# Batch 0's gate and up products as seven block products, with the weight sums made as the second slot opens

## The chip, the cores and the metric

The kernel runs on one core of a Trainium2 chip. The metric is the device time of one execution in microseconds (us), the median over several executions; smaller is better. PE is the matrix engine, PEld its weight loads, DVE the vector engine, ACT the scalar engine, POOL GpSimd, and SP the engine that issues most of the DMA transfers.

## The reference

A pre-norm block on four batches of 512 tokens, all in 32-bit floats: `x` is 4 x 512 x 512, 32 query heads and 8 key/value heads of 16, and a gated layer with 1376 hidden columns.

```python
x = x + attn(layernorm(x), Wq, Wk, Wv, Wo)    # rotary embedding, causal softmax, 4 query heads for a key head
x = x + ffn(layernorm(x), W_gate, W_up, W_down)

def ffn(x, W_gate, W_up, W_down):
    up = x @ W_up.T
    gate = silu(x @ W_gate.T)
    return gate * up @ W_down.T
```

## The kernel before

**Slots.** Attention is done in 32 groups (batch, one of four sets of heads, one of two halves), eight groups to a batch. `slot(b, steps)` runs the eight groups of batch `b`, and puts other work of PE, as steps with an estimated cost each, into gaps between the parts of a group: after each of four visits, and (from slot 1 on) after the group's `averages`. `fill` takes steps from the list until the slot's share is used up; a step of cost zero (`after`) rides along, so its place in the list is its place in every engine's queue. All engines run their instructions in the order of the program, SP too: a transfer that must wait holds up every transfer behind it.

**What stands in the gaps.** In slot 0: projections of the batches 1 to 3. In slot 1: the output projection and second layernorm of batch 0 (`attended(0)`), the last of the query projections of batch 3, then batch 0's gated layer and half of its down products. In slot 2: the rest of batch 0's down products, batch 1's output projection, batch 1's gated layer and half of its down products; in slot 3 the same for batch 2. What is left (batch 3) runs behind the last slot with nothing beside it: the tail.

**The gated layer, two ways.** The 1376 hidden columns are ten blocks of 128 (`whole = 10`) and an edge of 96. Batch 0 goes through `hidden`: for each block and each of gate and up, four products over the 512 inputs, 512 tokens wide; its weights come from `load_f`, two blocks ahead. The batches 1 to 3 go through `seven`: ten units, `u` even for gate and odd for up, each of 256 hidden columns x 512 inputs x 512 tokens, done with Strassen's scheme in Winograd's form, seven block products in place of eight. A unit has seven steps (`a1, y1, y2, v1, v2, w1, w2`), each with two products 256 tokens wide. It needs four sums of the activations (`sums_of`, DVE, into `sums`, which lies in `xnTs[1]`) and the weights in seven blocks (`packed[u]` in DRAM: three blocks copied as they are, four sums made from them). It adds its results together on DVE (L687, L696, L697, L705), and silu is a tanh on ACT (L666), a DVE step (L667) that `owed` puts into the next unit, and a product with up (L670; on POOL inside the slots, on DVE in the tail). `hidden` has instead a tanh and two DVE steps for each block (L561, L562, L564).

**The weight blocks.** `packs(u)` makes `packed[u]` in slot 1, beside batch 0's layer: `load` brings 512 KB to `spare` (in `xnTs[1]`) and copies the 384 KB of unchanged blocks from DRAM to DRAM (L587, L588); `combine` is four additions on POOL (L592 to L595); `store` writes 512 KB (L598). In slots 2 and 3 and in the tail a unit's blocks come by four loads (L621, 896 KB a unit), issued during the unit before.

**The edge and its moves.** The 96 last columns are done by `hidden` in all batches, for the batches 1 to 3 ahead of the units. Its last step moves three corners of 32 x 128 by SP (L566, `home<-home`), which wait for DVE's L564. `seven` puts all four sums between the edge's two halves.

**Inside the slots** `narrow` is set, and each product is cut into four strips of 32 output columns that run side by side on PE. The profile has two records for each of these matmuls: a 512-wide product is 8 records, a 256-wide one 8.

**Causal masking** of the exponentials is done by POOL (`causal`, L861) ahead of `averages` (L883) on PE; `greatest` (L801) on DVE has to read a score bank before PE writes it again (L755, L768).

Of the kernel before, what the change touches and what calls it, by code (L numbers as in the profile page):

```python
# [74 lines left out]
def preln_block_kernel(  # L75
# [52 lines left out]
    shared = flat[:, : 24 * P].rearrange("p (a b k m) -> p a b k m", a=3, b=2, k=NK)  # L128
    wq_sb = flat[:, : NK * D].rearrange("p (k m) -> p k m", k=NK)
    wk_sb, wv_sb = shared[:, 2, 0, :, :], shared[:, 2, 1, :, :]  # L130
# [36 lines left out]
    spare = turn.rearrange("p (u f m) -> p u f m", u=2, f=4)  # L167
    rest_w = rope_sb[:, : 2 * NK * 96].rearrange("p (a k m) -> p a k m", a=2, k=NK)
    once = rope_sb[:, 2 * NK * 96 : 2 * T]
# [330 lines left out]
    wgu = {}  # L500

    def load_f(c):

        if c >= NF or c in wgu:
            return
        f = c % NF
        n = min(P, FF - f * P)
        t = shared[:, (c + 2) % 3, :, :, :]
        for a, w in enumerate((wg, wu)):
            load_w(t[:, a, :, :n], w[:, f * P : f * P + n])  # L510
        wgu[c] = t

    def hidden(b, n, owed=None):

        gs = {}

        def half(f, a):
            def weights(a):
                return rest_w[:, a] if owed else wgu[f][:, a]

            m = min(P, FF - f * P)
            most = T - P
            cols = slice(0, T if m == P else most)

            def product(ps, k):
                if a == 0 and k == 0 and not owed:
                    load_f(f + 2)
                if m == P:
                    product_of(ps, weights(a)[:, k, :], xnTs[0][:, k, :], k == 0, k == NK - 1)
                    return  # L530


                for q in range(3):
                    at = slice(32 * q, 32 * q + 32)
                    nc.tensor.matmul(  # L535
                        ps[at, :most],
                        lhsT=weights(a)[:, k, at],
                        rhs=xnTs[0][:, k, :most],
                        start=k == 0,
                        stop=k == NK - 1,  # L540
                    )
                for q, kq in (divmod(n, NK) for n in range(3 * k, 3 * k + 3)):
                    nc.tensor.matmul(  # L543
                        ps[96:P, ts(q, P)],
                        lhsT=weights(a)[:, kq, 32 * q : 32 * q + 32],
                        rhs=xnTs[0][:, kq, most:],
                        start=kq == 0,
                        stop=kq == NK - 1,
                    )

            def finish(ps):
                return [(0.69, lambda: gated(ps))]

            def gated(ps):
                if owed:
                    owed()
                if a == 0:
                    gs[f] = scratch()

                    g = gs[f][:, cols]  # L560
                    nc.scalar.activation(g, ps[:, cols], AF.Tanh, scale=0.5)  # L561
                    nc.vector.scalar_tensor_tensor(g, g, 1.0, ps[:, cols], ALU.add, ALU.mult)  # L562
                else:
                    nc.vector.tensor_tensor(homes[n][:, f, cols], ps[:, cols], gs[f][:, cols], ALU.mult)  # L564
                    for q in range(3) if m < P else ():
                        nc.sync.dma_start(  # L566
                            out=homes[n][32 * q : 32 * q + 32, f, most:], in_=homes[n][96:P, f, ts(q, P)]
                        )

            return [(1.72 if m == P else 1.29, step) for step in portions([lambda ps, k=k: product(ps, k) for k in range(NK)], finish)]  # L570

        return [step for f in range(NF - 1 if owed else 0, NF) for a in range(2) for step in half(f, a)]
# [4 lines left out]
    def packs(u):  # L577
# [3 lines left out]
        t, columns = spare[:, u % 2], w.rearrange("(k p) m -> p k m", p=P)  # L581

        def load():
            for i in range(2):
                load_w(t[:, 2 * i : 2 * i + 2, :].rearrange("p f (k m) -> p (f k) m", k=2), w[:, at + P - P * i :][:, :P])
            raw = packed[u].rearrange("p f (k m) -> p (f k) m", k=2)
            nc.sync.dma_start(out=raw[:, :4, :], in_=columns[:, :, at + P : at + 2 * P])  # L587
            nc.sync.dma_start(out=raw[:, 4:6, :], in_=columns[:, 2:, at : at + P])  # L588
# [12 lines left out]

    def load_rest():
        for a, w in enumerate((wg, wu)):
            load_w(rest_w[:, a, :, :], w[:, whole * P :])


    places = {"a": (0, (0,)), "y": (256, (1, 3)), "v": (1280, (5, 6)), "w": (2304, (2, 4))}
# [8 lines left out]
    def load_blocks(kind, v):  # L616
        if v >= (B - 1) * whole:
            return
# [4 lines left out]
    def first_blocks():  # L623
        for kind in "ayvw":
            load_blocks(kind, 0)

    def sums_of():
# [3 lines left out]
        for out_, one, other in ((t3, b22, b12), (t1, b12, b11), (t2, b22, t1), (t4, b21, t2)):  # L631
            nc.vector.tensor_tensor(out_, one, other, ALU.subtract)  # L632

    def seven(b, n):
# [6 lines left out]
        def owed():  # L641
            while carried:
                carried.popleft()()
# [505 lines left out]
```

## Time and profile before

| what | us |
|---|---|
| three runs: median, lowest to highest | 865.3, 864.68 to 866.2 |
| the profiled execution: its time | 863.93 |
| its span, first to last instruction | 862.2 |
| DVE, ACT, POOL busy over the span | 535.9, 217.2, 292.5 |

The granted clock of PE was 0.999 of full speed over the span. The slots can be told in the trace by the groups of `averages` (L883): slot 0 ends at about 174 us, slot 1 at 357, slot 2 at 538, slot 3 at 710; then the tail runs to 862. "Busy" is the time in which an engine had at least one instruction running, and a wait is put down to what was released last.

```profile
L562 DVE SCALAR_TENSOR_TENSOR u<-u,mm 128x512 f32<-128x512 f32 x10 | 6.9, 688 | 14.9 <-ACT u L561 14.9
L705 DVE TENSOR_TENSOR u<-mm,u 128x512 f32<-128x512 f32 x15 | 10.3, 684 | 4.0 <-PE mm L269 2.9 <-PE mm L272 1.2
L697 DVE TENSOR_TENSOR u<-mm,u 128x256 f32<-128x256 f32 x15 | 6.4, 424 | 0.5
L670 POOL TENSOR_TENSOR home<-home,u 128x512 f32<-128x512 f32 x20 | 25.2, 1281 | 25.5 <-DVE u L705 25.3
L592 POOL TENSOR_TENSOR xnT<-xnT 128x256 f32<-128x256 f32 x10 | 7.3, 728 | 0.2
```

These are groups of instructions by line and shape: line, engine, operation, tiles (out<-in), shapes, count, then busy time, mean nanoseconds of one, and the idle time of the engine just before them with what ended it.

### The profile page before, as it was taken

What the parts mean: (1) busy time and instruction counts of PE and PEld (TensorE: products, weight loads), DVE (VectorE), ACT (ScalarE), POOL (GpSimd) and SP (SyncE); (2) the same over time, 40 slices, a digit from 0 to 9 for tenths busy, and PEclk for the clock granted to TensorE, in tenths of its full rate; (3) what the DMA queues carried; (4) which work ended last, traced back from release to release, by engine and by line L of the source; (5) the groups of instructions that cost most, each with busy time, mean ns of one, the idle gap of its engine ahead of it and who ended that gap; (6) DMA issues with size and microseconds to landing.
All of it is one profiled execution on the core that took longest, in us unless ns stands there. A gap on an engine that the chain in (4) does not pass through costs nothing.

```text
span 862.2 us, 26973 instructions
## 1 busy us (share of the span) xinstructions
PE 836.6 (97%) x11446; PEld 419.9 (49%) x11446; DVE 535.9 (62%) x1593; ACT 217.2 (25%) x296; POOL 292.5 (34%) x418
## 2 busy tenths in 40 slices
PE   6999999999999999999999999999999999999998
PEld 5654444544333335333655543334555544478843
DVE  7887788778555554467777774586777433256620
ACT  1034434422222222222332332222333420011100
POOL 4565565664343444222233341231233331000000
PEclk9999999999999999999999999999999999999999
DMA  8500114004866753534233320132432402445300
GB/s 255 135 6 4 53 17 88 5 4 106 285 185 194 201 174 107 182 114 107 62 116 103 91 87 14 64 52 76 121 102 89 131 15 73 104 138 152 105 12 36
DMA packets 134519, 85.50 MB, mean 99 GB/s; under 512 B 60320, under 2 KB 121376, under 8 KB 134144
## 3 DMA queue, kind: packets, MB, share of 16 engines
q1 hardware_dynamic: 134112, 78.02, 32.4%
q10 hardware_dynamic: 288, 5.77, 1.7%
q8 instruction: 90, 1.47, 0.7%
q14 instruction: 29, 0.24, 0.1%
HBM read 64.95 MB, written 22.54 MB: 101 GB/s over the span
## 4 chain that ended last, share of the span: by engine, by line
PE 76%; DVE 12%; POOL 3%; DMA 3%; issue 2%; ACT 2%; SPq 1%; POOLq 0%; DVEq 0%; ACTq 0%
PE mm L272 37%; PE mm L269 15%; PE sc L755 12%; DVE junk L801 7%; PE av L883 6%; PE sc L768 4%; POOL e L861 2%; PE mm L543 1%; ACT e L856 1%; DMA shared<-packed 1%; DVE rot L331 1%; DVE st L219 1%; PE mm L535 1%; DVE xnT L632 1%; DMA lowest<-turned 1%
## 5 line engine op out<-in xcount | busy, mean ns | idle before, releaser
L801 DVE CUSTOM_DVE_ANT_0 junk<-sc,mask 128x128 f32<-128x128 f32 (+3 forms) x512 | 251.1, 490 | 142.8 <-PE sc L768 83.8
L856 ACT ACTIVATE e<-sc 128x1024 f32<-128x1024 f32 (+1 forms) x192 | 165.4, 881 | 378.6 <-PE sc L768 308.4
L272 PE MATMUL mm<-xnT,shared 128*32 128x256 f32 (+1 forms) x3520 | 244.7, 420 | 1.4 <-DVE xnT L280 1.0
L861 POOL TENSOR_SCALAR_AFFINE_SELECT e<-e 128x512 f32<-128x512 f32 (+2 forms) x192 | 106.8, 566 | 269.5 <-ACT e L856 266.4
L272 PEld LDWEIGHTS mm<-xnT,shared 128*32 128x32 f32 x3520 | 117.0, 110 | 112.5 <-issue 61.8
L755 PE MATMUL sc<-home,qa 32*64 32x512 f32 (+6 forms) x2048 | 158.1, 421 | 6.1 <-DVE low L801 3.5
L768 PE MATMUL sc<-qa,home 32*64 32x512 f32 (+6 forms) x2048 | 152.3, 427 | 3.9 <-DVE low L801 3.3
L755 PEld LDWEIGHTS sc<-home,qa 32*64 32x64 f32 x2048 | 67.3, 131 | 94.9 <-issue 32.7
L272 PE MATMUL mm<-wd_sb,home 128*32 128x512 f32 (+1 forms) x808 | 93.7, 595 | 0.0
L883 PE MATMUL av<-e,home 128*32 128x512 f32 (+3 forms) x1024 | 82.3, 438 | 1.7 <-POOL e L861 1.6
L269 PE MATMUL mm<-xnT,shared 128*128 128x256 f32 x360 | 79.9, 382 | 1.9 <-DMA shared<-packed 1.9
L269 PEld LDWEIGHTS mm<-xnT,shared 128*128 128x128 f32 x360 | 68.0, 191 | 13.7 <-issue 4.5
L768 PEld LDWEIGHTS sc<-qa,home 32*64 32x64 f32 x2048 | 58.8, 130 | 28.5 <-DVE low L801 10.5
L269 PE MATMUL mm<-wd_sb,home 128*128 128x512 f32 (+1 forms) x150 | 65.0, 593 | 0.0
L724 DVE SCALAR_TENSOR_TENSOR xr<-mm,xr 128x512 f32<-128x512 f32 x16 | 11.0, 687 | 71.5 <-PE mm L269 54.9
L883 PEld LDWEIGHTS av<-e,home 128*32 128x32 f32 x1024 | 30.9, 109 | 47.0 <-issue 35.7
L272 PEld LDWEIGHTS mm<-wd_sb,home 128*32 128x32 f32 (+1 forms) x808 | 27.0, 110 | 50.6 <-issue 48.8
L269 PEld LDWEIGHTS mm<-wd_sb,home 128*128 128x128 f32 (+1 forms) x150 | 28.4, 190 | 35.8 <-issue 35.8
L272 PE MATMUL mm<-wo_sb,cx 128*32 128x512 f32 x384 | 44.9, 595 | 0.0
L801 DVE DVE_READ_ACCUMULATOR2_ANT low<- 128x1 f32 x512 | 42.3, 83 | 0.0
L222 POOL TENSOR_TENSOR rstd<-rstd,neghalf 128x1 f32<-128x1 f32 x32 | 20.4, 639 | 60.3 <-DVE rstd L221 59.8
L907 POOL TENSOR_TENSOR inv<-us,inverse 128x256 f32<-128x256 f32 x32 | 20.6, 645 | 49.6 <-DVE inverse L900 48.4
(112 smaller groups left out, 670.3 us busy)
## 6 DMA issues: line engine op xcount, KB each, us to landing
shared<-packed SPq DMA_DIRECT2D x90, 256.0 KB
flip<-u SPq DMA_DIRECT2D x88, 64.0 KB
packed<-xnT SPq DMA_DIRECT2D x10, 512.0 KB
xnT<-flip SPq DMA_DIRECT2D x18, 256.0 KB
xr<-in_x SPq DMA_DIRECT2D x16, 256.0 KB
out<-xr SPq DMA_DIRECT2D x16, 256.0 KB
shared<-packed SPq DMA_DIRECT2D x30, 128.0 KB
xa<-in_x SPq DMA_DIRECT2D x12, 256.0 KB
```

The costliest lines, as they stand in the source:

```text
L219: nc.vector.bn_stats(st, src)
L222: nc.gpsimd.tensor_tensor(rstd, rstd, neghalf, ALU.pow)
L269: nc.tensor.matmul(out, lhsT=lhsT, rhs=rhs, start=start, stop=stop)
L272: nc.tensor.matmul(out[c : c + 32], lhsT=lhsT[:, c : c + 32], rhs=rhs, start=start, stop=stop)
L724: nc.vector.scalar_tensor_tensor(xr[b, i], py[i], 0.5, xr[b, i], ALU.mult, ALU.add)
L755: nc.tensor.matmul(dst[at : at + 64, :n], lhsT=qa[g][rows_of(r), q : q + 64], rhs=keys_of(g)[rows_of(r), :n], start=True, stop=True,)
L768: nc.tensor.matmul(dst[at : at + 64, first_q:], lhsT=keys_of(g)[rows_of(r), k : k + 64], rhs=qa[g][rows_of(r), P * j + first_q :], start=True,
L801: nc.vector.tensor_tensor_reduce(out=junk[:, :n], in0=src, in1=mask[:, T - n : T] if i else mask[:, T:], scale=-1.0, scalar=BIG, op0=ALU.a ...
L856: nc.scalar.activation(dst, src, AF.Exp, scale=1.0 / math.sqrt(DH))
L861: nc.gpsimd.affine_select(out=e[rows, heads, c : c + P], in_=e[rows, heads, c : c + P], compare_op=ALU.is_ge, fill=0.0, base=base, pattern ...
L883: nc.tensor.matmul(av[32 * r : 32 * r + 32, P * j :], lhsT=v[:, j, 4 * (m // 2) + r, DH * (1 - hf) : DH * (3 - hf)], rhs=e[:, r, c : c + n ...
L907: nc.gpsimd.tensor_tensor(us[m][:, :, hf, :], turned[0][:, :, hf, :], by, ALU.mult)
```

## The change

1. Batch 0 goes through `seven` too. `hidden` and `load_f` are gone; the edge has a function of its own (`edge`), which comes behind the units for batch 0 and ahead of them for the others. Batch 0 keeps `once` in the unused last part of its home tile, since the other place still holds rotary tables.
2. The sums of weights have to be there earlier. The unchanged blocks are copied in slot 0 (`copies`, 20 transfers). `load`, `combine` and `store` start when slot 1 opens and follow a timetable (`timed`) of one pack in 4.5 units of estimated cost. They use `homes[0][:, 4:10]`, free after slot 0, three packs in turn, in place of `xnTs[1]`.
3. The four sums of activations are four steps, each between other steps; `owed` gives out one silu step at a time (in `y1` and in `v1`) in place of two in `y2`.
4. The edge's moves wait in a queue (`moves`) and are issued later: in step 12 of the units for the batches 1 to 3, in the down products for batch 0.
5. Places in the flat weight buffer are arranged anew, so that unit 0's `a` and `y` blocks can be loaded early in slot 1 and `v` and `w` behind the last query projection.

```diff
-    wk_sb, wv_sb = shared[:, 2, 0, :, :], shared[:, 2, 1, :, :]
+    wk_sb, wv_sb = (flat[:, n * NK * P : (n + 1) * NK * P].rearrange("p (k m) -> p k m", k=NK) for n in (4, 5))
...
-    spare = turn.rearrange("p (u f m) -> p u f m", u=2, f=4)
...
-    def load_f(c):
...
-    def hidden(b, n, owed=None):
...
+    moves = deque()
+
+    def moved():
+        while moves:
+            moves.popleft()()
+
+    def edge(n):
+        home, f, most, gs = homes[n], whole, T - P, []
+
+        def product(ps, a, k):
...
+        def gated(ps, a):
+            if a == 0:
+                gs.append(scratch()[:, :most])
+                g = gs[0]
+                nc.scalar.activation(g, ps[:, :most], AF.Tanh, scale=0.5)
+                nc.vector.scalar_tensor_tensor(g, g, 1.0, ps[:, :most], ALU.add, ALU.mult)
+                return
+            nc.vector.tensor_tensor(home[:, f, :most], ps[:, :most], gs[0], ALU.mult)
+            for q in range(3):
+                moves.append(
+                    lambda q=q: nc.sync.dma_start(
+                        out=home[32 * q : 32 * q + 32, f, most:], in_=home[96:P, f, ts(q, P)]
+                    )
+                )
...
     def packs(u):
-        t, columns = spare[:, u % 2], w.rearrange("(k p) m -> p k m", p=P)
+        t = homes[0][:, 4 + 2 * (u % 3) : 6 + 2 * (u % 3), :].rearrange("p a (f m) -> p (a f) m", m=2 * P)
         def load():
...
-            raw = packed[u].rearrange("p f (k m) -> p (f k) m", k=2)
-            nc.sync.dma_start(out=raw[:, :4, :], in_=columns[:, :, at + P : at + 2 * P])
-            nc.sync.dma_start(out=raw[:, 4:6, :], in_=columns[:, 2:, at : at + P])
...
+    def copies(u):
+        at = 2 * P * (u // 2)
+        columns = (wg, wu)[u % 2].rearrange("(k p) m -> p k m", p=P)
+        raw = packed[u].rearrange("p f (k m) -> p (f k) m", k=2)
+        nc.sync.dma_start(out=raw[:, :4, :], in_=columns[:, :, at + P : at + 2 * P])
+        nc.sync.dma_start(out=raw[:, 4:6, :], in_=columns[:, 2:, at : at + P])
...
-    places = {"a": (0, (0,)), "y": (256, (1, 3)), "v": (1280, (5, 6)), "w": (2304, (2, 4))}
+    places = {"v": (0, (5, 6)), "w": (1024, (2, 4)), "y": (2048, (1, 3)), "a": (3072, (0,))}
...
-    def sums_of():
+    def sums_of(which):
         t1, t2, t3, t4 = (sums[:, n] for n in range(4))
-        for out_, one, other in ((t3, b22, b12), (t1, b12, b11), (t2, b22, t1), (t4, b21, t2)):
-            nc.vector.tensor_tensor(out_, one, other, ALU.subtract)
+        one, two, by = ((t1, b12, b11), (t2, b22, t1), (t3, b22, b12), (t4, b21, t2))[which]
+        nc.vector.tensor_tensor(one, two, by, ALU.subtract)
...
     def seven(b, n):
+        once = rope_sb[:, 2 * NK * 96 : 2 * T] if b else home[:, whole, : 2 * P]
         def owed():
-            while carried:
+            if carried:
                 carried.popleft()()
...
-        edge = hidden(b, n, owed)
-        return [*edge[:2], after(sums_of), *edge[2:], *steps]
+        t = [after(lambda s=s: sums_of(s)) for s in range(4)]
+        if b == 0:
+            return [t[0], t[1], steps[0], t[2], steps[1], t[3], *steps[2:], *edge(n)]
+        ends = edge(n)
+        return [ends[0], t[0], ends[1], t[1], ends[2], t[2], ends[3], t[3], *steps[:12], after(moved), *steps[12:]]
...
+    early = [*rest1[16:-8], *turns, begin3, *rest2, *turned3, *rest3[:-24]]
+    for u in range(whole):
+        early.insert(4 * u + 4, after(lambda u=u: copies(u)))
+    slot(0, early)
...
+    tiles[3:3] = [after(moved)]
+    cut += 1
...
+    asides = []
+    for u in range(whole):
+        load, combine, store = packs(u)
+        asides += [(max(4.5 * u - 2.5, 0.2 * u), load), (4.5 * u + 5, combine), (4.5 * u + 8, store)]
+    start1 = [before[0], *rest3[-24:-12], *before[1:], *rest3[-12:-1], *behind, rest3[-1]]
+    layer = seven(0, 0)
+    blocks = [after(lambda kind=kind: load_blocks(kind, 0)) for kind in "vw"]
+    asides += [(13.0, lambda: load_blocks("a", 0)), (13.0, lambda: load_blocks("y", 0))]
+    layer = [*layer[:8], after(spilled), *layer[8:36], after(load_rest), after(load_down), *layer[36:]]
+    slot(1, timed([*start1, *blocks, *layer, *tiles[:cut]], asides))
```

`timed(steps, asides)` puts each aside ahead of the first step at which the summed cost has reached its time. The units of the batches 1 to 3, their loads and the slots 2 and 3 are otherwise as they were.

## The prediction, made before the changed kernel ran

> **What bounds the kernel now.** I read the busy times of the whole page first, then the same by slot, then what PE waited for, then the blocks in which the changed products run.
>
> ```profile
> PE 836.6 (97%) x11446; PEld 419.9 (49%) x11446; DVE 535.9 (62%) x1593; ACT 217.2 (25%) x296; POOL 292.5 (34%) x418
> ```
> ```profile
> core 0: us, PE busy (x) PEld busy (x) DVE busy (x) ACT busy (x) POOL busy (x), PEclk, DMA share, GB/s
> 174.30:357.20 182.90, 180.45 (x2502) 69.59 (x2504) 105.76 (x345) 48.44 (x60) 81.95 (x121) 1.00 0.53 159
> 357.20:538.20 181.00, 180.70 (x2980) 85.54 (x2976) 122.32 (x369) 50.55 (x69) 52.23 (x78) 1.00 0.32 94
> 538.20:710.20 172.00, 168.99 (x2788) 82.44 (x2784) 108.49 (x305) 50.00 (x69) 51.31 (x75) 1.00 0.29 81
> 710.20:862.20 152.00, 146.31 (x576) 93.11 (x566) 59.44 (x100) 9.51 (x21) 3.51 (x5) 1.00 0.31 88
> ```
>
> These rows are slot 1, slot 2, slot 3 and the tail. PE is the bound in all: slot 1, which the change rebuilds, has it busy for 180.45 of 182.90 us. Slot 2 already runs a layer by `seven` inside the gaps and loses only 0.3 us. So PE time taken from slot 1 shortens the run, unless a wait comes in its place. What PE waits for, in slot 1 (first fence) and from 538 us on (second):
>
> ```profile
> PE av L883 <- POOL e L861: 1.2, 3, 0.5
> PE mm L272 <- DVE xnT L280: 1.0, 1, 1.0
> ```
> ```profile
> PE mm L269 <- DMA shared<-packed: 1.9, 1, 1.9
> PE sc L768 <- DVE low L801: 1.7, 1, 1.7
> PE sc L755 <- DVE low L801: 0.8, 2, 0.4
> ```
>
> Each line: total us, times, longest. All of them lie at places that the change touches.
>
> **Step 1, the products: -8.2 us.** Four blocks of the timeline, two of each kind (start, us, form, records):
>
> ```profile
> 223.90 1.93 PE L272 MATMUL mm<-xnT,shared 128*32 128x512 f32 x16
> 226.80 3.64 PE L272 MATMUL mm<-xnT,shared 128*32 128x512 f32 x32
> 428.23 2.80 PE L272 MATMUL mm<-xnT,shared 128*32 128x256 f32 x48
> 435.67 3.66 PE L272 MATMUL mm<-xnT,shared 128*32 128x256 f32 x64
> ```
>
> Sixteen more records of 512 columns (two products) cost 3.64 - 1.93 = 1.71 us; sixteen of 256 (one step of a unit) 3.66 - 2.80 = 0.86. What a block has beyond that (0.22) is paid once for each gap, and the number of gaps stays. `hidden` has 10 blocks x 2 x 4 products x 8 records = 640 records: 40 x 1.71 = 68.4 us. `seven` has 10 x 7 steps of 16: 70 x 0.86 = 60.2. The edge and the down products are the same. The shorter products load as many weights for half the columns; slot 2 does just that at the pace above, PEld at 85.54 of 181 us, so I add nothing.
>
> **Step 2, DVE and ACT in slot 1: no cost beside PE, but for the opening.** Taken out: ten L562 and ten L564 of 0.688 us, 13.8. Put in, by the rows of slots 2 and 3: ten each of L687, L696, L705 (0.687, 0.688, 0.684) and L697 (0.424), 24.8; ten L667 (0.768), 7.7; four sums (0.68 to 0.80), 3.0. DVE goes from 105.8 to about 127.5 us in a slot of some 178: 72%, beside 68% in slot 2. ACT gets ten tanh (0.622) in place of ten (0.597), and ten copies to `once` (0.364): +3.9 on 48. The cover is PE's own time; without it all of DVE's 21.7 would count.
> At the opening of the layer the cover is thin. After `averages` DVE has L897 and L900 (0.68 + 0.25), then two sums (1.4) that `y2` needs, 2.3 us, while PE has two steps (1.8): 0.5 of wait. `v1` stands behind a third step and a score block (2.8 + 1.04 = 3.8 us), and its weights are issued only when the last query projection has read the buffer and `lowest` has gone, some 1.5 us in: with a landing like the tail's (3.29, below) 4.8, with the 4.55 of 656.3 us in the chain of waits 6.1. I take 1.2 for both together; bounds 0 (SP early) and 2.3. In turn, L280's 1.0 goes: the transposed tiles are now needed one gap later, behind `averages`.
>
> **Step 3, POOL: +3.6 us.** The packs' four additions are as many as before, but come closer together, and ten products L670 (1.28 us each, 12.8) join them in slot 1: about 95 of 178 us. The total is harmless; the place is not. One group of slot 1 before, on POOL, and PE behind it:
>
> ```profile
> 282.06 1.91 POOL L861 TENSOR_SCALAR_AFFINE_SELECT e<-e 128x512 f32<-128x512 f32 x3 [8.41 <-ACT e L856]
> 284.06 0.73 POOL L592 TENSOR_TENSOR xnT<-xnT 128x256 f32<-128x256 f32 x1
> 286.48 0.73 POOL L595 TENSOR_TENSOR xnT<-xnT 128x256 f32<-128x256 f32 x1
> 287.16 0.76 POOL L861 TENSOR_SCALAR_AFFINE_SELECT e<-e 128x256 f32<-128x256 f32 x2
> ```
> ```profile
> 287.62 0.77 PE L883 MATMUL av<-e,home 128*32 128x256 f32 x6 [0.50 <-POOL e L861]
> ```
>
> Mask, a combination (284.06 to 287.21), the last mask, and PE waits 0.50. In the changed program's order three groups have a combination at this place: pack 4 as here (0.5); pack 1 in the group with two rstd steps (the mask at 194.17 comes about 1.0 later, on top of 0.21: 1.2); and pack 7 with both products of unit 1 ahead of it, 2 x 1.28 = 2.56 more: 3.1. Sum 4.8, less the 1.2 of now: +3.6. Bounds: -1.2 (no mask late) and three times 3.1 less 1.2 = +8.1. Behind the late mask stands only `qa` for the group after next.
> [...]
>
> **Step 4, SP and the transfers.** Slot 0 gets 20 DRAM copies of 0.62 us issue each, in its first three groups. SP idles there (54.8 to 66.3 us and 70.5 to 82.4, between `qa` and `lowest`), eight copies (5 us) fit in each; the last four delay the `xa` loads at 86.84 by 2.5 us: landed at 92.0 (2.68 as at the start), first read at 93.46. Nothing; without that cover some 1 us on DVE. In slot 1 SP has by its order: store of pack u, loads of a later pack, and a unit's blocks between them. A unit takes 7 steps, 10 us with the attention between, and its blocks are asked for a unit ahead. Landing takes 3.3 to 4.6, a store waits for POOL up to 3.2. That fits. The load in the stretch of packs, units and the spill together will be about that of 215 to 235 us now (DMA share 0.81 to 0.90), where PE lost nothing. I take 0; bounds 0 and the second rival.
> [...]
>
> **Step 5, moves and sums in the later layers: -2.9 us.** In the tail SP stood at the moves until DVE's L564 was done, and only then asked for unit 1's blocks (SP's timeline, then the chain of waits):
>
> ```profile
> 759.53 1.84 SPq L566 DMA_DIRECT2D home<-home  x3
> ```
> ```profile
> 762.62 3.29 DMA shared<-packed
> ```
>
> PE stood until 766.04, the 1.9 above. With the moves 12 steps later SP is free from 753.6 (after `out`), `a` waits only for `a1` at about 758.3 and lands before 764.1: -1.9 (bounds -1.9 and 0). The 1.7 in slot 3 (600.3 us) follows four sums in one run (596.8 to 600.2) ahead of `greatest`. Now a PE step lies between any two, but two or three still fall in one gap: -1.0, bounds 0 and -2.5 (all waits for L801 there). `owed` one by one makes the same work smoother, 0.
>
> **Sum.** -8.2 - 1.0 + 1.2 + 3.6 - 1.0 - 1.9 = -7.3. Against the profiled execution: 863.9 - 7.3 = 856.6. Its time is 1.4 below the median of the runs; with that, 858.0.
>
> **Rivals.**
> *All cover holds* (for it: slot 2 loses 0.3 us with the same units): no new waits, 865.3 - 8.2 - 1.0 - 1.2 - 2.5 - 1.9 = 850.5. Against it: slot 2 has no packs on POOL.
> *SP becomes the bound in slot 1: slower.* Packs 4 to 9 are still under way while units run. A block load stands behind a store that waits for POOL (3.2 here) and a pack load that waits for an older store to land; the longest wait of SP for a stored pack is now 7.7 us. 3.2 + 7.7 + a landing of 3.3 is 14.2 against 10 us of lead: 4 us for a unit. With four units late, 16 on -7.3: 874. It decides against the kernel once the lead is missed by more than 1.8 us in each of four units. Against it: 7.7 was seen once, beside the 2.5 MB of down weights, which now come after the packs.
> *DVE becomes the bound:* each of the four groups with units pays a wait like slot 3's 1.7: +6.8, 864.8, no change. For it: 77% busy (16.87 of 22 us) from 446 to 468 us. Against it: PE lost 0.27 there.
> *Strassen is not in effect for batch 0, or costs 8 products:* then only steps 3 to 5 remain, about 866. The program's order shows the 70 steps, so it gets next to nothing.
>
> **How the numbers follow.** Forecast 0.72, all cover 0.10, SP 0.11, DVE 0.07, the last under 0.01. Faster by over 0.2% (1.7 us, about what a measurement of this kernel can tell from no change) are the first two: 0.82; slower is the SP case, 0.11; same is DVE's, 0.07. The likeliest case's own range is 854 to 862. To leave out no more than 2 in 10 I reach to 853 (into the case of full cover) and 863.5 (POOL near its upper bound, or half of DVE's case).
>
> **What would show it.** Right: no records of 512 columns for mm<-xnT,shared in narrow strips, 70 steps at 0.86; slot 1 at about 178.5 us (182.9 - 8.2 - 1.0 + 1.2 + 3.6); PE's wait for L861 in slot 1 at 3 to 5 us, the largest in the group where L670 and a combination meet; no wait of L269 for `packed` in the tail. Wrong: PE waiting for `packed` in slot 1 over 2 us, waits for L801 in slot 1 over 3 us, a slot 0 longer than 174.3, or slots 2 and 3 changed by more than 3.

## The result, and the profile after

The changed kernel takes 872.8 us (median; 872.54 to 875.07) against 865.5 us of the kernel before on the same chip: a ratio of 1.009, with a 95% interval of 1.0071 to 1.0109. The forecast was 858.0 us with a range from 853 to 863.5, so the sign was wrong. The profiled executions are 8.8 us apart (872.76 and 863.93, spans 871.05 and 862.22).

First the same view by slot as before: slot 1, slot 2, slot 3 and the tail, cut at the end of each slot's last `averages`.

```profile
core 0: us, PE busy (x) PEld busy (x) DVE busy (x) ACT busy (x) POOL busy (x), PEclk, DMA share, GB/s
176.14:370.94 194.80, 177.39 (x2981) 88.60 (x2984) 128.29 (x379) 51.06 (x70) 97.04 (x130) 0.97 0.48 147
370.94:551.88 180.94, 180.64 (x2980) 85.51 (x2976) 121.93 (x369) 50.55 (x69) 52.67 (x78) 1.00 0.32 94
551.88:721.14 169.26, 168.74 (x2789) 82.27 (x2784) 106.91 (x305) 50.02 (x69) 50.53 (x75) 1.00 0.30 83
721.14:871.05 149.91, 146.05 (x574) 93.14 (x566) 59.48 (x100) 9.39 (x21) 3.51 (x5) 1.00 0.31 89
```

Cut at the same places, the kernel before has 182.65, 180.95, 172.10 and 152.00 us. So slot 0 is 1.6 us longer, slot 1 12.2 longer, slot 2 the same, slot 3 2.8 shorter and the tail 2.1 shorter: together 8.8. The whole loss is in slot 1, and its row has a column to look at that the prediction never used: PEclk is 0.97 there and 1.00 everywhere else.

What PE waited for in slot 1 (waits: total us, times, longest):

```profile
PE mm L269 <- DMA shared<-packed: 11.7, 5, 5.1
PE av L864 <- POOL e L842: 4.6, 3, 2.8
PE mm L269 <- DVE xnT L608: 1.0, 1, 1.0
```

In the same stretch the kernel before waited 1.2 us for the mask and 1.0 for L280. From 551 us to the end only one line is left, where there were three with 4.4 us:

```profile
PE sc L736 <- DVE low L782: 0.4, 1, 0.4
```

PE's timeline around the longest waits of slot 1 (start, us, form, records, idle before and its end):

```profile
221.50 1.42 PE L864 MATMUL av<-e,home 128*32 128x256 f32 x8 [2.77 <-POOL e L842]
222.32 3.41 PE L269 MATMUL mm<-xnT,shared 128*32 128x256 f32 x32
...
243.34 1.93 PE L269 MATMUL mm<-xnT,shared 128*32 128x256 f32 x32 [2.83 <-DMA shared<-packed]
248.00 2.84 PE L269 MATMUL mm<-xnT,shared 128*32 128x256 f32 x32 [2.73 <-DMA shared<-packed]
...
286.63 1.93 PE L269 MATMUL mm<-xnT,shared 128*32 128x256 f32 x32
293.70 3.37 PE L269 MATMUL mm<-xnT,shared 128*32 128x256 f32 x32 [5.14 <-DMA shared<-packed]
```

Read the waits at the right, and then the durations. The same 32 records take 1.93 us, also right behind the wait of 2.83 us, but 3.41, 2.84 and 3.37 us behind the other three. The clock shows why (windows over the block behind the wait at 221.5 and over the one at 293.7):

```profile
222.00:225.00 3.00, 3.00 (x34) 1.72 (x32) 1.99 (x3) 0.32 (x1) 2.92 (x3) 0.50 0.29 87
...
294.00:297.00 3.00, 3.00 (x32) 1.38 (x24) 0.00 (x0) 0.37 (x1) 0.00 (x0) 0.56 0.61 214
```

Each of these three times the granted clock falls to a half for some 3.4 us, which by 3.413 x 0.5 costs 1.7 us of work each time. In windows of ten us, slot 1 has 0.83 (220 to 230), 0.94 and 0.89 (240 to 260) and 0.83 (290 to 300): 0.51 x 10 = 5.1 us in all.

Why not behind the wait of 2.83 us? By the trace's clock records the three stretches at half clock last 3.413 us each and start at 221.57, 248.88 and 293.25 us: 8 and 13 times 3.413 us apart. Here are windows cut on that grid, around the waits of 2.83 us (240.51 to 243.34) and 2.73 us (245.28 to 248.00):

```profile
238.64:242.05 3.41, 1.87 (x52) 0.92 (x43) 3.25 (x9) 1.02 (x1) 0.28 (x1) 1.00 0.91 265
242.05:245.46 3.41, 1.93 (x32) 1.12 (x32) 1.09 (x7) 0.00 (x0) 1.56 (x3) 1.00 1.07 378
245.46:248.88 3.42, 0.88 (x17) 0.67 (x21) 0.56 (x1) 0.00 (x0) 2.71 (x3) 1.00 0.58 172
248.88:252.29 3.41, 3.41 (x52) 1.90 (x44) 0.00 (x0) 0.37 (x1) 2.64 (x4) 0.50 0.98 316
```

The first wait is shared by two windows, and PE was idle for 45 and 43% of them. The second lies almost wholly in one, idle for 74%, and the half clock follows that one. In this profile, then, the idle share of such a window tells the two waits apart, and their lengths do not (more under the hardware, at the end).

Now slot 1 adds up. PE's busy time less these 5.1 us is 172.3 against 180.2 before: the products save 7.9 of the 8.2 us forecast (6.8 in e6 below, where no half clock has to be taken off). The waits are 17.4 us (all gaps over 60 ns) against 2.4: +15.0. Then -7.9 + 15.0 + 5.1 = +12.2, the measured difference.

Where the block loads were held up stands in the chain of waits (start, us, what):

```profile
226.17 5.53 DMA shared<-packed
231.78 10.51 DMA spill<-wd_sb
242.35 5.52 DMA shared<-packed
...
280.20 10.67 DMA wd_sb<-in_wd
290.94 2.63 DMA shared<-packed
```

Two large transfers lie under the two places with the longest waits: the spill of batch 3's tile (2.8 MB, one transfer on ACT's queue, L1050) and the load of the down weights (2.5 MB, one transfer on SP's, L1054; the line here is that of its small rest, 192 KB, issued right behind it). The chain doesn't show the block load that had to run beside the spill. By the trace's landing records it was issued at 233.15 us and landed at 243.21, after 10.1 us, and PE waited for it until 243.34. The 5.5 us of the chain are loads that landed just before the spill started and that were issued as it landed; the one issued at 290.94 us, when the down weights had landed, took 2.63. But SP's queue was late as well, by this view of its own waits from 176 to 372 us:

```profile
SPq L569 <- POOL home L566: 11.1, 3, 5.7
SPq L174 <- DMA packed<-home: 10.5, 3, 3.6
SPq L601 <- DMA wd_sb<-in_wd: 5.7, 1, 5.7
```

Three times SP stood about 3.5 us at a pack's load, until the store of three packs earlier had landed (they share a place), and once 5.7 us at a block load, until the down weights had landed (in the trace that load, issued at 290.43 us, is the eighth transfer behind the down load of 278.54, and tells of its landing by the same semaphore). It also stood at three pack stores until POOL had combined (185 to 191, 237 to 239 and 264 to 268 us). So two theories are to be told apart. *Bulk*: the large transfer itself makes the block loads beside it late. *Queue*: SP, which issues them in order, is held up by pack stores and by the down load.

### The profile page after: what moved, and what is told of

It is laid out like the page before. It is cut to its first block, busy times and chain, and to the rows that moved or that the text cites. A ratio compares the mean times of both kernels' runs of the same rounds, so it can differ in the third digit from the quotient of the medians.

```text
span 871.0 us, 28040 instructions
## 1 busy us (share of the span) xinstructions
PE 834.2 (96%) x11926; PEld 439.3 (50%) x11926; DVE 556.9 (64%) x1627; ACT 219.7 (25%) x306; POOL 307.5 (35%) x428
## 3 DMA queue, kind: packets, MB, share of 16 engines
q8 instruction: 94, 1.54, 0.7%
## 4 chain that ended last, share of the span: by engine, by line
PE 74%; DVE 10%; DMA 6%; POOL 5%; issue 2%; ACT 1%; SPq 1%; POOLq 0%; DVEq 0%; ACTq 0%
PE mm L269 33%; PE mm L266 18%; PE sc L736 11%; DVE junk L782 7%; PE av L864 6%; PE sc L749 4%; POOL e L842 2%; DMA shared<-packed 2%; PE mm L519 2%; DMA wd_sb<-in_wd 1%; DMA spill<-wd_sb 1%; ACT e L837 1%; PE mm L511 1%; DVE rot L328 1%; POOL rot L329 1%
## 5 line engine op out<-in xcount | busy, mean ns | idle before, releaser
L269 PE MATMUL mm<-xnT,shared 128*32 128x256 f32 x4000 | 240.3, 385 | 12.6 <-DMA shared<-packed 11.7
L842 POOL TENSOR_SCALAR_AFFINE_SELECT e<-e 128x512 f32<-128x512 f32 (+2 forms) x192 | 106.2, 563 | 263.6 <-ACT e L837 257.1
L269 PEld LDWEIGHTS mm<-xnT,shared 128*32 128x32 f32 x4000 | 135.3, 111 | 110.3 <-issue 44.5
L647 POOL TENSOR_TENSOR home<-home,u 128x512 f32<-128x512 f32 x30 | 37.7, 1277 | 36.1 <-DVE u L683 36.0
L643 ACT ACTIVATE u<-home 128x512 f32<-128x512 f32 x40 | 23.0, 623 | 65.3 <-DVE home L683 61.6
```

The costliest lines, as they stand in the source:

```text
L269: nc.tensor.matmul(out[c : c + 32], lhsT=lhsT[:, c : c + 32], rhs=rhs, start=start, stop=stop)
L643: nc.scalar.activation(t, g, AF.Tanh, scale=0.5)
L647: engine.tensor_tensor(g, g, t, ALU.mult)
L842: nc.gpsimd.affine_select(out=e[rows, heads, c : c + P], in_=e[rows, heads, c : c + P], compare_op=ALU.is_ge, fill=0.0, base=base, pattern ...
```

## The experiments

Each time stands against runs of the kernel before on the same chip (medians 865.6 to 866.7 us).

**e1: the spill in eleven pieces.**

```diff
-    def spilled():
-        nc.scalar.dma_start(out=spill, in_=homes[3])
+    def spilled(f):
+        nc.scalar.dma_start(out=spill[:, f, :], in_=homes[3][:, f, :])
...
-    layer = [*layer[:8], after(spilled), *layer[8:36], after(load_rest), after(load_down), *layer[36:]]
+    for f in reversed(range(NF)):
+        layer.insert(8 + 2 * f, after(lambda f=f: spilled(f)))
+    layer = [*layer[:47], after(load_rest), after(load_down), *layer[47:]]
```

> The spill of batch 3 (2.8 MB in one transfer on ACT's queue) goes out as eleven transfers of 256 KB, one at every second product step. Theory 'bulk': the one large transfer holds the sixteen DMA engines, and block loads that are issued beside it land late (5.5 us instead of some 3.3); then the stalls of 2.83 us (at 240.5) and 2.73 us (at 245.3) go, and with them the stretch at half clock that follows (1.7 us): 872.8 - 7.3 = 865.5 us. Theory 'queue': SP is late because it stands still 3.5 us at a time for the landing of older pack stores (at 214.5, 219.5 and 242.7); these waits do not depend on the spill, both stalls stay within 1 us, and the time is 871 to 873 us.

876.3 us, ratio 1.0115 (1.010 to 1.013): neither theory's time. The profiled executions are 2.9 us apart, of which slot 1, the only one that the edit touches, has 0.2; 0.9 stand in slot 0 and 1.9 in slot 3, where PE waited 1.69 us for a block load. So the waits tell more than the time. The 2.83 and 2.73 us for block loads are gone; what is left near there is 0.57 us at 229. SP's waits are just what they were (from 205 to 250 us):

```profile
SPq L174 <- DMA packed<-home: 11.0, 4, 4.2
```

So SP's standing for pack stores does not by itself make a block load late: bulk, for these two waits. The landing records agree: the load issued at 233.50 us in this run landed after 3.0 us, its counterpart in the changed kernel after 10.1. In their place stands a wait of 4.83 us of `av` at 249 us, 2 us more than either of them. POOL's timeline in this run shows it:

```profile
245.84 1.92 POOL L842 TENSOR_SCALAR_AFFINE_SELECT e<-e 128x512 f32<-128x512 f32 x3 [6.77 <-ACT e L837]
247.85 2.51 POOL L647 TENSOR_TENSOR home<-home,u 128x512 f32<-128x512 f32 x2
250.31 0.73 POOL L563 TENSOR_TENSOR home<-home 128x256 f32<-128x256 f32 x1
...
252.73 0.72 POOL L566 TENSOR_TENSOR home<-home 128x256 f32<-128x256 f32 x1
253.40 0.77 POOL L842 TENSOR_SCALAR_AFFINE_SELECT e<-e 128x256 f32<-128x256 f32 x2
```

Between the first masks (L842) and the last one, POOL does two products (L647) and a pack's four combining steps (L563 to L566), 5.6 us. The prediction had priced exactly this meeting (at 3.1 us). In the changed kernel it is there too, but PE stood waiting for a block load in that time: a wait that was hidden under another, and shows when the first is taken away.

**e2 and e3: the load of the down weights on another queue, or in pieces.**

```diff
-        load_w(wd_sb[:, :whole, :], wd[: whole * P, :])
+        nc.scalar.dma_start(out=wd_sb[:, :whole, :], in_=wd[: whole * P, :].rearrange("(k p) m -> p k m", p=P))
```
```diff
+    def load_down(f):
+        n = min(FF - f * P, 2 * P)
+        if n == 2 * P:
+            load_w(wd_sb[:, f : f + 2, :], wd[f * P : f * P + n, :])
+        else:
+            nc.sync.dma_start(out=wd_sb[:n, f, :], in_=wd[f * P :, :])
...
+    for n in reversed(range(6)):
+        layer.insert(36 + 6 * n, after(lambda f=2 * n: load_down(f)))
```

> The load of the down weights (2.5 MB, one transfer) is issued on ACT's queue instead of SP's, at the same place in the program. Theory 'queue': SP stood still 5.73 us (284.7 to 290.4) for the landing of this very load, because the ninth transfer after it takes its semaphore again; on ACT's queue nothing of SP waits for it, the stall of 5.14 us at 288.6 goes with the half clock after it (1.7 us): 872.8 - 6.8 = 866.0 us. Theory 'bulk': the block loads share the DMA engines with the same bytes, the stall stays over 3 us and the time is 870 to 873 us.

> The load of the down weights stays on SP's queue and is cut into five transfers of 512 KB (and the rest of 192 KB), six product steps apart. Both theories, bulk and queue, expect the stall of 5.14 us to go with its half clock, to 866 us; if 512 KB are still enough to hold a block load back, waits of 1 to 2 us appear at one or more of the five places and the time is 868 to 871 us. With e2 it tells what the transfer's size does from what its queue does.

e2: 873.0 us (1.007, 1.0045 to 1.0095). The wait is 3.83 us instead of 5.14, with half clock behind it still. e3: 867.4 us (1.001, 0.9994 to 1.0025; the profiled execution is a quick one, 864.3); no block load is waited for there at all, only 0.5 us for `low`. PE's waits from 280 to 372 us, e2 in the first fence and e3 in the second:

```profile
PE mm L269 <- DMA shared<-packed: 3.8, 1, 3.8
```
```profile
PE av L864 <- POOL e L842: 0.6, 1, 0.6
PE mm L269 <- DVE low L782: 0.5, 1, 0.5
```

With the load on ACT's queue nothing of SP waits for its landing directly, and three quarters of the wait stay: that is the transfer's size. It works through SP's order all the same: even `lowest`, 16 KB, took 6.8 us to land beside it, and SP stood 4.0 us for that before it issued the block loads. The other 1.3 us may be the queue's, but the run moves the load a little too. Cutting the transfer removes the wait on the same queue, which both theories expected. So size and order make this wait together, and the size is what can be cut.

**e4: the combining steps apart.**

```diff
-        asides += [(max(4.5 * u - 2.5, 0.2 * u), load), (4.5 * u + 5, combine), (4.5 * u + 8, store)]
+        asides += [(max(4.5 * u - 2.5, 0.2 * u), load), (4.5 * u + 8, store)]
+        asides += [(4.5 * u + 5 + 0.9 * n, lambda n=n, combine=combine: combine(n)) for n in range(4)]
```

> A pack's four combining steps on POOL are issued 0.9 us of product time apart instead of in one row of 3 us; the work is the same. Theory 'order': av waits for the mask because a row of four stands ahead of it; the mask then waits for one step (0.74 us) at most, the waits of av in slot 1 (1.26 and 2.77 us) fall under 0.7 us each and the half clock after 221.5 (1.7 us) goes: 872.8 - 2.6 - 1.7 = 868.5 us. Rival 'load': POOL is full between 185 and 230 us (9.7, 8.5, 5.0, 9.2 and 9.6 of each 10 us), the wait moves to another group and keeps its sum of 4 us: 871.5 to 873 us.

873.5 us (1.0075, 1.006 to 1.009): no gain alone. The waits of `av` did fall, from 1.26 and 2.77 us to 0.14, 0.43 and 1.54, and the half clock between 220 and 230 us went. But PE then came to the layer's opening earlier and waited 1.79 us there for DVE's sums (0.96 in the changed kernel) and 1.23 for `low`, and the down load's wait grew to 7.44 us. Both theories have a part: the order of POOL's work makes the wait, and DVE, 7.7 and 8.5 us busy of ten from 210 to 230 us, stands right behind it.

**e5: one part undone in batches 1 to 3.**

```diff
+            if at_once:
+                moved()
...
-        ends = edge(n)
-        return [ends[0], t[0], ends[1], t[1], ends[2], t[2], ends[3], t[3], *steps[:12], after(moved), *steps[12:]]
+        ends = edge(n, at_once=True)
+        return [*ends[:2], t[2], t[0], t[1], t[3], *ends[2:], *steps]
```

> One part of the change undone, in batches 1 to 3 only: the four weight sums are issued in one place behind the second step of the edge again (order t3, t1, t2, t4), and the three small transfers of the edge at once. Theory 'waits': the sums stood 1.70 us before a pair of scores and 0.40 us before the next in slot 3 (the pieces that are gone after the change), the small transfers 1.94 us in the tail; all of it comes back and nothing else: 872.8 + 1.7 + 0.4 + 1.9 = 876.8 us (1.0046 of the changed kernel, 1.0135 of before). On record these terms stood at 1.0 and 1.9, which would be 875.7. Rival 'alignment': the waits went because the layers begin at another point of the stream; then it stays at 872 to 873.5 us.

880.1 us (1.0164, 1.0143 to 1.0185), 7.3 us over the changed kernel where 4.0 were expected. A wait of 1.7 us for `low` came back where it was in slot 3, and one of 2.2 us in the tail; a block load in slot 3 is waited for too (551 us to the end):

```profile
PE mm L266 <- DVE home L646: 2.2, 1, 2.2
PE mm L269 <- DMA shared<-packed: 1.8, 1, 1.8
PE sc L751 <- DVE low L784: 1.7, 1, 1.7
PE sc L738 <- DVE low L784: 0.4, 1, 0.4
```

That is 6.1 - 0.4 = 5.7 us, and behind the 2.2 us in the tail the clock is 0.77, 0.50 and 0.88 in the windows of two us from 780 to 786 us: 1.7 more. Together 7.4. But the 1.8 us for a block load (at 673 us) are not the undoing's: nine of the twelve other kernels with the change's later layers wait 0.8 to 1.7 us at that place, the changed kernel's profile happens not to. So the separate sums and the late moves do what they are for, and their absence costs more than the wait they leave.

**e8: both large transfers cut up** (the edits of e1 and e3).

> Both large transfers cut up (spill in eleven on ACT's queue, down weights in six on SP's), combining as in the change. Theory 'bulk plus hidden wait': the stalls for block loads are gone but for about 1 us, and the wait of av for the mask behind the two products and the four combining steps, which lay hidden behind the stall for the block load at 245 us, shows as 4.8 us at 249 us; stalls of slot 1 about 11 us (17.4 in the changed kernel) and two stretches at half clock instead of three: 872.8 - 6 - 1.7 = 865 us, equal to before. Rival 'queue': SP's waits for pack stores are untouched, 868 to 871 us.

869.3 us (1.0045, 1.0028 to 1.0063). The waits of slot 1 were forecast well: 12.5 us (about 11 expected), of which 5.18 for the mask at 249.5 us and only 0.58 for a block load. The time was not: the clock was low for longer than I took (0.83 in 40 to 50 us, 0.83 in 220 to 230, 0.66 in 250 to 260), 6.8 us in place of 3.4. Behind this wait of 5.18 us the clock was low for twice 3.4 us; behind the 5.14 of the changed kernel for one.

**e6: e8 and e4 together.**

> e8 and e4 together: both large transfers cut up, and each pack's four combining steps issued 0.9 us of product time apart. Theory 'two covers': of the wait of 4.8 us at 249 us at most 1.5 are left, stalls of slot 1 about 8 us, none of them long enough for a half clock: 872.8 - 9.4 - 5.2 = 858 us, 0.991 of before. Rival 'load' (POOL and DVE are simply full between 205 and 260 us, and a wait that is taken away comes back at the next group): 863 to 866 us.

862.0 us (0.9956, 0.9941 to 0.9971): faster than before. The wait of 5.18 us is gone; in the profiled execution slot 1 has 8.6 us of waits, and the clock stays at 1.00 in all of it. It is 4 us over the forecast, 2.88 of them a block load at 241 us that was not expected. So each edit alone gained little or lost, because the next wait stood right behind; together they give 10.8 us against the changed kernel's median.

**e7, e9: the packs spread further, or loaded later.** e7 is e6 with 5.4 in place of 4.5 in the three places of the timetable; pack 9 is then staged in planes that batch 0's unit 4 uses for its result, so batch 0's output is not the reference's. e9 is e6 with loads at 4.5u - 0.5 instead of 4.5u - 2.5.

```diff
-        asides += [(max(4.5 * u - 2.5, 0.2 * u), load), (4.5 * u + 8, store)]
+        asides += [(max(5.4 * u - 2.5, 0.2 * u), load), (5.4 * u + 8, store)]
```
```diff
-        asides += [(max(4.5 * u - 2.5, 0.2 * u), load), (4.5 * u + 8, store)]
+        asides += [(max(4.5 * u - 0.5, 0.2 * u), load), (4.5 * u + 8, store)]
```

> e6 with the ten packs 5.4 instead of 4.5 us of product time apart: the same transfers and the same combining work, spread to 1.2 of the length. If the load of POOL and of the DMA engines in 205 to 260 us makes what is left in e6, 2 to 4 us less than e6, about 855 us; if the order of the work makes it, equal to e6 within 1 us; if the packs come too late for their units (pack 9's store stands at 56.6 us of product time, its unit's loads at about 65), new waits of the products for block loads towards the end of the slot and a time over e6's.

> e6 with every pack load issued 2 us of product time later (4.5u - 0.5 instead of 4.5u - 2.5), so that SP reaches it when the store three packs earlier has landed. In e6 SP still stood 3.7, 3.6, 0.7 and 1.7 us for such landings between 213 and 240 us, and the product then waited 2.88 us at 241 us for a block load that stands behind the last of them. Theory 'queue' (for what is left in e6): these stands and the 2.88 us go, 862.0 - 2.9 = 859 us. Rival: the loads come 2 us nearer to their combining steps, POOL waits for them in front of a mask, and av waits as long as the product did: 862 to 864 us.

e7: 866.0 us (0.9997, 0.9981 to 1.0013), 4 us over e6. DVE waits in it for POOL and for a pack's store (2.3 and 1.7 us) because packs and units now share planes; this run does not tell load from order. e9: 867.4 us (1.0014, 1.0000 to 1.0027). The theory of SP's queue fell: its stands at 213 and 218 us are gone, but the wait at 241 us grew to 4.26 us. (SP now stood 6.7 us at stores that wait for POOL, from 205 to 250 us, 2.8 in e6; so its queue isn't cleared of all blame.) The windows show the engines full at that place, as in e6 (1.01):

```profile
240.00:250.00 10.00, 5.74 (x96) 3.04 (x92) 2.67 (x10) 1.20 (x3) 5.73 (x7) 0.83 1.03 345
```

The last two numbers are the DMA engines' share (full) and GB/s.

**e10: the later loads alone,** on the changed kernel.

```diff
-        asides += [(max(4.5 * u - 2.5, 0.2 * u), load), (4.5 * u + 5, combine), (4.5 * u + 8, store)]
+        asides += [(max(4.5 * u - 0.5, 0.2 * u), load), (4.5 * u + 5, combine), (4.5 * u + 8, store)]
```

> The changed kernel with the later pack loads of e9 alone: both large transfers whole, combining in a row. Theory 'queue': SP's stands for pack stores made the block loads late, so the stalls of 2.83 and 2.73 us at 240 to 248 us fall under 1 us each without the spill being touched, and a half clock with them: 865.5 us. Theory 'bulk': the spill still lies over the loads of unit 1, the stalls keep at least 4 of their 5.6 us: 870 to 873 us.

877.5 us (1.0132, 1.0119 to 1.0146). It decides less than hoped: the two waits at 240 and 245 us became one of 3.40, which is between the two theories' figures, and POOL now waited 4.4 us for a pack's load in front of a mask, so `av` waited 7.42 us at 218 us. Later loads are simply worse.

**e12: the spill's pieces later than in e6** (and the down weights' too).

```diff
-        extra.setdefault(8 + 2 * f, []).append(lambda f=f: spilled(f))
+        extra.setdefault(26 + 2 * f, []).append(lambda f=f: spilled(f))
-        extra.setdefault(36 + 6 * n, []).append(lambda n=n: load_down(2 * n))
+        extra.setdefault(42 + 6 * n, []).append(lambda n=n: load_down(2 * n))
```

> e6 with the spill's eleven pieces from product step 26 to 46 of the layer instead of 8 to 28, and the down weights' six pieces from step 42 to 72 instead of 36 to 66: out of the stretch in which the packs are still loaded and stored. In e6 the DMA engines are full from 240 to 250 us (share 1.01) and the product waits 2.88 us there. Theory 'bulk': with the spill's pieces out of the way the share from 240 to 250 us falls under 0.9, the 2.88 us go to under 1, and the time is 859 to 860 us. Rival 'queue': that block load is late because it stands behind SP's wait of 1.65 us for a pack store; the wait stays over 2 us and the time is 861.5 to 863 us.

863.5 us (0.9967, 0.9954 to 0.9981), no better than e6. But it tells the theories apart once more. The wait at 241 us went from 2.88 us (for a block load) to 0.82 (for `low`), and a new wait of 3.07 us for a block load came at 283 us, where the pieces now are. The windows of e12:

```profile
240.00:250.00 10.00, 8.84 (x162) 5.15 (x158) 6.14 (x23) 2.48 (x4) 7.47 (x12) 1.00 0.69 218
...
280.00:290.00 10.00, 6.93 (x156) 3.90 (x148) 5.54 (x16) 2.27 (x4) 3.14 (x3) 1.00 0.96 305
```

In e6 the share from 240 to 250 us was 1.01. The wait went where the bytes went.

**e11: the later layers' part alone**, on the kernel before: batch 0 keeps its 512-column products.

```diff
-        edge = hidden(b, n, owed)
-        return [*edge[:2], after(sums_of), *edge[2:], *steps]
+        ends = hidden(b, n, owed)
+        t = [after(lambda s=s: sums_of(s)) for s in range(4)]
+        return [ends[0], t[0], ends[1], t[1], ends[2], t[2], ends[3], t[3], *steps[:12], after(moved), *steps[12:]]
```

> The kernel before with one part of the change alone: batch 0 keeps its 512-column products, and batches 1 to 3 get the four sums apart, the steps owed one at a time and the small transfers of the edge late. By the stalls that are gone in slot 3 (3.01 to 0.52) and in the tail (1.94 to 0): -4.4 us, 0.995 of before, 862.0 us where before is 866.4. By the terms on record (1.0 and 1.9): -2.9, 863.5 us. If the gain came from batch 0's part shifting the stream against the waits: no difference from before.

859.9 us (0.9927, 0.9913 to 0.9942), the best of all kernels run here, 6.8 us under before where 4.4 were expected. The waits from 538 us on fall from 4.9 to 1.3 us, 3.6 us. About 2 us of the rest go with the clock: twelve of the seventeen executions of before beside it show a mean granted clock of 0.997 or 0.998 and take 865.7 to 867.3 us, the five at 0.999 or 1.000 take 864.2 to 865.4; e11's four are all at 0.999 or 1.000. That the waits of 1.70 and 1.94 us in before cause its lower clock fits this, but was not tried by itself. Against the five quick ones alone the gain is still 4.9 us, 1.3 more than these waits; that stays open.

Batch 0's part, then, costs about 13 us on top of e11 (872.8 against 859.9), though it takes 8 us of work from PE. Even with the three edits of e6 it gains nothing over e11 (862.0): slot 1 takes 182.1 us in e6 and 182.65 before, 6.8 us less work of PE against 6.2 us more waits. That e6 is faster than before is mostly the later layers' doing (slot 3 and the tail are 3.3 us shorter).

## Why the prediction was wrong, step by step

| term | forecast, us | measured, us |
|---|---|---|
| products | -8.2 | -7.9 (PE busy in slot 1, half clock taken off) |
| L280's wait | -1.0 | -1.0 |
| opening of the layer | +1.2 | +1.3 (0.96 for the sums, 0.38 for a block) |
| POOL ahead of the mask | +3.6 | +3.4 (1.26 + 2.77 + 0.58, less 1.2) |
| SP and transfers in slot 1 | 0 | +11.3 (2.83 + 2.73 + 5.14 + 0.57) |
| half clock behind waits | not named | +5.1 |
| sums in slot 3 | -1.0 | -2.8 |
| moves in the tail | -1.9 | -2.1 |
| slot 0 | 0 | +1.6 |

The measured column sums to +8.9; the spans differ by 8.8. Steps 1, 2 and 5 held, with step 5's sums taken too small: 2.1 of the bound of 2.5 came, and the rest of the 2.8 is mostly a wait for a block load that comes and goes (0.4 before, none here, 0.8 to 1.7 in nine of the eleven experiments with these later layers). Step 3's sum came out partly by luck, for its places were right only in part: the largest wait is in the group with the two rotary steps (217 us), and the meeting of L647 with a combination, expected to be the worst, lay under a DMA wait until e1 uncovered it. Of slot 0's 1.6 us, 0.6 are waits; 0.9 stand already at 59 us, and two experiments that share all of slot 0 with the changed kernel lie 1.6 us apart at the same place (58.65 in e10, 60.27 in e8). At its end the twelve profiles that share it stand between 174.6 and 177.3 us, so the 1.6 are not shown to be the change's.

**The step that failed** is step 4: "That fits. The load in the stretch of packs, units and the spill together will be about that of 215 to 235 us now (DMA share 0.81 to 0.90), where PE lost nothing. I take 0". The load was not far off (a share of 0.99 from 230 to 240 us and 0.95 from 280 to 290). The conclusion was. Beside the down weights the engines were as full before as after (first line before, second after: PE busy is the second number, the DMA share the last but one):

```profile
275.00:285.00 10.00, 10.00 (x164) 3.82 (x160) 4.82 (x18) 2.65 (x3) 2.71 (x5) 1.00 0.97 314
280.00:290.00 10.00, 8.56 (x168) 4.18 (x156) 8.48 (x24) 3.82 (x6) 1.01 (x2) 1.00 0.95 303
```

PE lost nothing there *because of who was waiting*. Before, batch 0's weights were asked for two feature blocks ahead (16 products, 13.7 us, with the attention between). The load issued at 272.67 us, beside the down weights, landed only after 11.5 us, at 284.13 by the trace's landing records; PE asked for it at 290.3, 17.6 us after its issue, so nothing of that could be seen. A unit's blocks are asked for one unit ahead at most, and `a` has only one place, free after `a1`: the load issued at 242.35 us landed 5.5 us later, at 247.9, and PE had been waiting for it since 245.3. The same share of the same engines was free of charge with one lead and cost 11 us with the other. And the two transfers of 2.8 and 2.5 MB, which take 10.5 and 11.8 us, were counted as load on average and not as ten us in which the block loads beside them land late (10.1 us beside the spill, 8.3 beside the down weights); e1, e3 and e12 show that they, cut and moved, take the waits with them.

**The second rival** came to 874 us with the sign right and the size close, but not for its reason. It expected 4 us in each of four units from SP standing at pack stores. SP did stand, 10.5 us in all; e1 has 11.0 us of it without the waits. So its agreement with 872.8 is mostly chance. One of its numbers was misread, too: a store waited for POOL 2.1 us at most before, not 3.2 (and 5.7 after). It was given 0.11.

**What was missing altogether** is that a wait of PE can cost more than itself. The price of a stall was put at its length everywhere; 5.1 us of half clock behind three waits were added in the changed kernel.

## What to carry to other kernels

When a change shortens the lead with which data is asked for, a stretch where "the DMA engines were just as full and nothing was lost" proves nothing: compare landing time with lead, for the longest transfer that can lie beside it, and cut transfers of megabytes into pieces (a block load landed after 10.1 us beside 2.8 MB in one transfer, after 3.0 beside its pieces). A wait that goes can uncover another that lay under it, so edits that fail one by one can work together (e1 +3.5 us, e4 +0.7, e3 -5.4 against the changed kernel's 872.8; all three 862.0), and still not pay for the part that they mend (859.9 without it). And look at the granted clock slot by slot: here stalls of 2.18 to 5.18 us on the matrix engine had 1.7 to 3.4 us of lost clock behind them, though not all (none right behind 2.83, 2.88 and 3.10).

## What the runs showed of the hardware

- **The clock.** After some idle times of PE the granted clock was 0.50 for about 3.4 us: after 2.77, 2.73 and 5.14 us here, after 2.18 in e5's tail (0.50 from 782 to 784 us); 5.18 in e8 was followed by twice as much (0.66 from 250 to 260 us). But after 2.83 us (at 240.5), 2.88 (e6) and 3.10 (e7) it was not at once: in e6 and e7 it was 1.00 in each ten us from 230 to 260. On the grid of 3.413 us that the three stretches of the changed kernel's profile lie on, the windows just ahead of them were idle for 81, 74 and 100%, and the one ahead of the half clock at the program's end (870.1 us) for 85%. No other window from 13.4 us on, where the clock records begin, was idle for more than 45%. In the kernel before, on the same grid laid from its one half clock, at the end (861.31 us), the most were 48% twice (598.49 to 601.90 and 762.33 to 765.74), with the clock at 1.00 behind both. What idle shares between 48 and 74% do, these two profiles do not show. One low stretch, 0.83 from 40 to 50 us in e8, where PE was busy for 8.90 of the ten, stays unexplained.
- **Issuing was slower beside the spill.** A transfer's issue on SP in the changed kernel mostly took 0.4 to 0.5 us (median 0.498 of 578); while the spill was under way (231.8 to 242.3 us) three in a row took 1.25 to 1.4 us, and SP fell behind by that too. (A store's 2.61 us there hold a wait of 1.4 for POOL.)
- **POOL beside DVE.** From 226 to 229.5 us, while DVE was busy without a gap, three combining steps took 1.06 to 1.17 us instead of 0.73. The last three of DVE's four sums, beside them, took 0.99 to 1.22 us; the median of all the sums in this run is 0.69.
